# Products of zeros on TensorE, a broadcast of B written twice, and a second sum placed behind it, in a four-layer state-space network

## The chip, the cores and the metric

The kernel runs on one core of a Trainium2 chip. The metric is the device time of one execution in microseconds. The engines are TensorE (PE for matmuls, PEld for its weight loads), VectorE (DVE), ScalarE (ACT), GpSimd (POOL) and SyncE (SP), which issues the DMAs. Each engine takes its instructions in order.

## The reference, cut to what matters

Four layers, each a mixer with a residual and a small feed-forward network with a residual, run over four images of 64 x 64 tokens with 96 channels. The mixers of layers 1 to 3 are selective scans: from the image come 192 channels, read in four orders (rows, columns, and both backwards), and for each channel `d` of each order `k` there are 16 states `n`. Per layer:

```python
x_dbl = einsum('bkdl,kcd->bkcl', xs, x_proj_weight)
dts, Bs, Cs = split(x_dbl, [R, R + N], axis=2)
delta = softplus(einsum('bkrl,kdr->bkdl', dts, dt_projs_weight) + bias)
...
def step(h, inp):
    u_l, dl, b_l, c_l = inp
    dA = exp(dl[..., None] * A)
    h = dA * h + (dl * u_l)[..., None] * b_l[:, :, None, :]
    y = einsum('bkdn,bkn->bkd', h, c_l)
    return (h, y)
...
ys = ys + Dp * u
```

`b_l` and `c_l` depend on the order and the state, and not on the channel. The sum over `n` in `y` is a sum of 16 products. Around it stand a projection in, a 3 x 3 convolution, a layer norm, a gate and a projection out. Layer 0's mixer is another recurrence; the feed-forward networks quantise to 8 bits.

## The kernel before, in words

The kernel has three parts one after the other: layer 0 (`gated`, L1120), the scans of layers 1 to 3 (`scans`, L902), and the last image's end. The scans are the long part: 3 layers x 4 images make 12 stages, and a stage has 24 items: 2 directions x 4 segments of `T` = 1024 tokens x 3 chunks of 128 channels. An item has 16 tiles, one for each state, of 128 channels x 1024 tokens. That makes 288 items and 4608 tiles.

For each tile `k` the functions inside `scans` do this:

- `c_rows` (L931): two DMAs on SP's queue spread a row of C over 64 partitions each, into one of six `c` buffers.
- `decays` (L941): ScalarE takes the exponential, into `da`.
- `b_rows` (L947): TensorE spreads the row of B over 128 partitions, by two bf16 matmuls of 96 rows x 512 columns with the constant selector `sel`, into one of two PSUM buffers `bc` (`wide`, L136).
- `times_b` (L956): VectorE multiplies `du` into `bc`, in place.
- `scan` (L961): VectorE runs the recurrence along the tokens, into one of four `h` buffers.
- `carry` (L975): ScalarE keeps the last column for the next segment.
- `times_c` (L981): POOL multiplies `h` into `c`, in place.
- `accumulate` (L1001): TensorE adds the product to the item's sum `acc` in PSUM, by `add_quarters` (L986): four f32 matmuls, each on a quarter of the array. The trace shows each f32 matmul as two records, so eight a tile. The first state of an item first opens the sum with another such set. There is one `acc` buffer; `take` (L1012) copies it out on ScalarE, and `store` writes it to memory.

The loop (L1042) goes over pairs of tiles, `a` = 2j and `b` = 2j + 1; `m` is the pair's place in its item, 0 to 7. `InOrder` (L80) keeps each engine's instructions in the order in which the program gives them, so what is written first on an engine is first in its queue; all of its instructions show line L91. It also counts TensorE's work in `pe.columns`: columns streamed, an f32 matmul counted four times, a matmul on part of the array counted for its share (`columns`, L68).

Side work is the rest of the network: the projections of the items to come (`prepare_chunk`, `prepare_segment`) and, as `Job`s, the stretch between two layers of the next image. These are generators, and `beside` (L1072) moves them on twice in each pair, within a limit of columns (`PACE`, L77).

TensorE's queue in one pair is so: the sums of tiles `a - 4` and `b - 4`, the side work, the broadcast for `a + 2`, the broadcast for `b + 2`. On VectorE: `times_b(a)`, side work, `times_b(b)`, `scan(a)`, side work, `scan(b)`. A broadcast for `a + 2` may be written only when `scan(a)` has read the same buffer. The loads of C for `a + 2` and `b + 2` go into the buffers that the sums of `a - 4` and `b - 4` have read:

```python
for k in (a - 4, b - 4):
    if 0 <= k <= last:
        accumulate(k)
    if k + 6 <= last:
        c_rows(k + 6)
```

Of the kernel before, what the change touches and what calls it, by code (L numbers as in the profile page):

```python
# [12 lines left out]
BF16 = mybir.dt.bfloat16  # L13
# [13 lines left out]
MM = 512  # L27
# [10 lines left out]
NB3 = 96  # L38
# [35 lines left out]
    return n / (max(1, 128 // max(rows, 32)) * max(1, 128 // max(cols, 32)))  # L74


PACE = (2.0, 1600), (2.2, 1800), (2.6, 2000)  # L77


# [37 lines left out]
def metaformer(ctx: ExitStack, tc: tile.TileContext, x, l0_ab, l0_rest, ssm, ffn, out):  # L117
    nc = tc.nc
    pe, act, dve, pool, sp = (
        InOrder(tc, e) for e in (nc.tensor, nc.scalar, nc.vector, nc.gpsimd, nc.sync)  # L120
    )
# [6 lines left out]
    def sb(bufs, tag, shape, dtype=F32):  # L128
        return pools[bufs].tile(shape, dtype, tag=tag, name=tag)

    def const(name, shape, dtype=F32):
        return pools[1].tile(shape, dtype, name=name)
# [3 lines left out]
    def wide():  # L136
        return wides[0].tile([128, T], F32, tag="bc", name="bc")
# [11 lines left out]
    def settle():  # L149
        banks["free"] += banks["back"]  # L150
        banks["back"] = 0
# [20 lines left out]
    def drain(chain, others=lambda: None, until=lambda: False):  # L172

        while chain is not None and not chain.done and not until():
            if not pump(chain):
                others()
            settle()
# [16 lines left out]
    sel = const("sel", [NB3, NS, 128], BF16)  # L194
    for n in range(NS):
        for k in range(2):
            at = NS * k + n
            dve.tensor_copy(
                sel[:, n, 64 * k : 64 * k + 64], mod32[:, at : at + 1].to_broadcast([NB3, 64])
            )  # L200

    fold = const("fold", [128, 32])
    dve.tensor_tensor(fold, ident[:, 0:32], ident[:, 32:64], ALU.add)
# [9 lines left out]
    for layer in range(4):  # L213
# [8 lines left out]
        b = const(f"b_{layer}", [128, 3 + C])  # L222
# [538 lines left out]
    def slot():  # L761

        load["now"] = max(0, min(load["now"], 4 * load["most"]) - load["most"])
# [102 lines left out]
    def prepare_chunk(item):  # L866

        w, sg = weights[item.layer].w, item.sg
        i = 3 * item.d + item.chunk
        bias = w[:, W_DTB + i : W_DTB + i + 1]  # L870
        f = w[NB3 : NB3 + 2 * R, W_IN + 128 * i : W_IN + 128 * (i + 1)]


        delta, du = sb(2, "delta", [128, T]), sb(2, "du", [128, T])
        for k in range(2):
            cols = slice(k * MM, (k + 1) * MM)
            ps = bank("dt_proj")
            pe.matmul(ps, f, sg.rows[NB3 : NB3 + 2 * R, cols], start=True, stop=True)
            yield
            act.activation(delta[:, cols], ps, AF.Identity, bias=bias)  # L880
            release()
            yield k == 0
        act.activation(delta, delta, AF.Softplus)
        exp_and_ln()
        yield
        yield
        pool.tensor_tensor(du, delta, sg.us[item.chunk], ALU.mult)
        item.delta, item.du = delta, du
# [13 lines left out]
    def scans(stages, jobs, pac):  # L902
# [16 lines left out]
        tiles = [(i, n) for i in items for n in range(NS)]  # L919
        last = len(tiles) - 1  # L920
# [10 lines left out]
        def c_rows(k):  # L931
            i, n = tiles[k]
            c = live[k, "c"] = sb(6, "c", [128, T])
            for half in range(2):
                row = NS * half + n
                sp.dma_start(
                    out=c[64 * half : 64 * half + 64],
                    in_=i.sg.cs[row : row + 1, :].to_broadcast([64, T]),
                )
# [4 lines left out]
            at = (3 * i.d + i.chunk) * NS + n  # L944
            act.activation(da, i.delta, AF.Exp, scale=weights[i.layer].decay[:, at : at + 1])

        def b_rows(k):  # L947
            i, n = tiles[k]
            b = live[k, "b"] = wide()
            for half in range(2):  # L950
                cols = slice(half * MM, (half + 1) * MM)
                pe.matmul(
                    b[:, cols], sel[:, n, :], i.sg.bs[:, cols], start=True, stop=True
                )
# [31 lines left out]
        def add_quarters(i, v, lhs, start, stop):  # L986

            for k in range(2):
                for j in range(2):
                    p = slice(64 * j, 64 * j + 64)  # L990
                    o = 64 * (j ^ k)
                    pe.matmul(
                        i.acc[o : o + 64, j * MM : (j + 1) * MM],
                        lhs[p],
                        v[p, k * MM : (k + 1) * MM],
                        start=start,
                        stop=stop,
                        tile_position=(64 * j, o),
                    )

        def accumulate(k):  # L1001
            i, n = tiles[k]
            h = live.pop((k, "c"))
            if n == 0:
                i.acc = pac.tile([128, T], F32, tag="acc", name="acc")
                if i.d == 0:
                    add_quarters(i, i.sg.us[i.chunk], weights[i.layer].skip[:, i.chunk, :], True, False)
                else:
                    add_quarters(i, i.yf, stacked, True, False)
            add_quarters(i, h, stacked, False, n == NS - 1)  # L1010

        def take(i):  # L1012
            i.y = sb(2, "y", [128, T])
            act.copy(i.y, i.acc)
# [13 lines left out]
        for k in range(2):  # L1028
            c_rows(k)
            b_rows(k)  # L1030
# [10 lines left out]
        half = NS // 2  # L1041
        for j in range(len(tiles) // 2 + 2):  # L1042
            q, m = divmod(j, half)
            a, b = 2 * j, 2 * j + 1
            on = b <= last
            if on:
                item = items[q]
                nxt = at(q + 1)
                if m == 0:
                    if q % per == 0:  # L1050
                        item.im.y = dram.tile([3, 128, L], F32, tag="y", name="y")
                        working += jobs[q // per]
                    chain = None
                if m == 2 and nxt is not None:
                    if item.chunk == 2:
                        drain(segment, work, lambda: nxt.sg.steps)
                    chain = Chain(prepare_chunk(nxt), True)
                if item.chunk == 1 and m == 1 and at(q + 2) is not None:
                    if q % per == per - 2:
                        for job in jobs[q // per][:1]:  # L1060
                            while not job.done:
                                job.step()
                                settle()
                    segment = Chain(next_segment(items[q + 2 : q + 5]))
                if m == 4 and nxt is not None:
                    start(nxt)
                    if nxt.d == 1:
                        nxt.yf = sb(2, "y", [128, T])
                        t = slice(nxt.seg * T, (nxt.seg + 1) * T)
                        sp.dma_start(out=nxt.yf, in_=nxt.im.y[nxt.chunk, :, t])  # L1070

            def beside(n):  # L1072
                slot()
                pumped(chain)
                pumped(segment)
                if n == 13:
                    drain(chain, work)
                    if item.chunk == 2:
                        drain(segment, work)
                work(True)  # L1080
                settle()

            if on:
                decays(b)
            for k in (a - 2, b - 2):
                if 0 <= k <= last:
                    carry(k)
            if a + 2 <= last:
                decays(a + 2)
            if 0 <= b - 2 <= last:  # L1090
                times_c(b - 2)
                del live[a - 2, "h"], live[b - 2, "h"]
            for k in (a - 4, b - 4):
                if 0 <= k <= last:
                    accumulate(k)
                if k + 6 <= last:
                    c_rows(k + 6)
            if on:
                times_b(a)
            beside(2 * m)  # L1100
            if on:
                times_b(b)
                scan(a)
            beside(2 * m + 1)
            if a + 2 <= last:
                b_rows(a + 2)
            if on:
                times_c(a)
                scan(b)
            if b + 2 <= last:  # L1110
                b_rows(b + 2)
            if m == 1 and q >= 1:
                take(items[q - 1])
                store(items[q - 1])
# [241 lines left out]
    with tc.tile_pool(name="pbig", bufs=2, space=bass.MemoryType.PSUM) as wides_pool:  # L1356
# [5 lines left out]
        for at in range(len(stages)):  # L1362
            jobs.append([])
            if at + 1 < len(stages):
                im, layer = stages[at + 1]
                jobs[-1].append(Job(between(im, layer - 1), *PACE[layer > 1]))

            for im in {10: images[:2], 11: images[2:3]}.get(at, ()):
                jobs[-1].append(Job(between(im, 3, im.dst), *PACE[2]))
        with tc.tile_pool(name="pac", bufs=1, space=bass.MemoryType.PSUM) as pac:  # L1370
# [121 lines left out]
```

## Time and profile before

| | |
|---|---|
| three runs | 19366.18, 19418.11, 19423.85 us; median 19418.11 |
| the profiled execution's time | 19356.33 us |
| its span, first to last instruction | 19354.5 us |
| mean granted TensorE clock | 0.823 |
| layer 0, scans, end (us from the span's start) | 0 to 1704, 1704 to 19041, 19041 to 19355 |
| granted clock in these | 0.94, 0.82, 0.52 |
| busy, share of the span | PE 77%, DVE 90%, ACT 55%, POOL 70% |
| busy in the scans, of 17337 us | PE 13076, DVE 16205, ACT 9846, POOL 12711 us |
| loads of C | 9216, issue to landing 4.5 us |
| SP's wait for TensorE's sums | 8929.2 us, 2964 times |

The groups of instructions give the busy time of each operation and the idle time of its engine just before it, with what ended most of that. The waits give the same by pairs of waiter and releaser. The busy time in given stretches has the granted clock of each. The order of time gives start and duration, with instructions of one kind merged (x2 is two of them, from the first one's start to the last one's end).

### The profile page before, as it was taken

To read this page: it belongs to the slowest core of one execution; us is meant where nothing else is said; L and a number is where in the kernel's file an instruction comes from. 1 tells how busy PE (TensorE), PEld (TensorE's weight loads), DVE (VectorE), ACT (ScalarE), POOL (GpSimd) and SP (SyncE) were. 2 spreads that over 40 slices of the span, in tenths; PEclk is the share of its full clock that TensorE was granted. 3 is DMA by queue.
4 is the path that set the end of the run, shared out by engine and by line. 5 is a ranking of instruction groups with operands and counts; after the bars stand their busy time and mean duration, and the time that the engine had idled before them with its cause. 6 is when DMAs were issued, how large, how long until landed. Compare 5 with 4: busy or idle time off the path is not lost.

```text
span 19354.5 us, 236828 instructions
## 1 busy us (share of the span) xinstructions
PE 14811.6 (77%) x75584; PEld 4774.9 (25%) x75584; DVE 17417.6 (90%) x13768; ACT 10683.2 (55%) x17977; POOL 13500.1 (70%) x9220
## 2 busy tenths in 40 slices
PE   8897776776777777777777777777777777777777
PEld 3332121221222222222222222222222222222224
DVE  7668999999999999999999999999999999998994
ACT  3444565565555565565565565565565565565554
POOL 3435777777777777777777777777777777777774
PEclk9898887887887787787887887787887887787876
DMA  2123676676677667667677677667667677677773
GB/s 54 49 60 99 171 189 171 173 189 169 177 191 179 174 179 182 174 180 186 173 181 182 173 182 180 170 180 183 173 180 182 173 180 182 172 182 177 180 179 92
DMA packets 1269928, 3193.12 MB, mean 165 GB/s; under 512 B 440336, under 2 KB 440560, under 8 KB 1262544
## 3 DMA queue, kind: packets, MB, share of 16 engines
q1 hardware_dynamic: 1268688, 3177.97, 64.7%
q8 instruction: 609, 9.98, 0.2%
q14 instruction: 631, 5.17, 0.1%
HBM read 2818.51 MB, written 308.28 MB: 162 GB/s over the span
## 4 chain that ended last, share of the span: by engine, by line
issue 35%; PE 22%; DVE 20%; ACT 6%; DMA 4%; POOL 3%; SPq 1%; POOLq 0%; DVEq 0%; ACTq 0%
DVE h L91 13%; PE acc L91 11%; DVE bc L91 5%; PE bc L91 4%; POOL c L91 2%; PE y_t L91 2%; ACT L91 2%; PE dt_proj L91 1%; DMA c<-cs 1%; ACT da L91 1%; ACT u L91 1%; PE out_proj L91 1%; DVE st L91 1%; SPq L91 1%; DMA u<-u 1%
## 5 line engine op out<-in xcount | busy, mean ns | idle before, releaser
L91 POOL TENSOR_TENSOR c<-h,c 128x1024 f32<-128x1024 f32 (+1 forms) x4992 | 11281.7, 2276 | 4576.5 <-DVE h L91 1847.5
L91 DVE TENSOR_TENSOR_SCAN h<-da,carry,bc 128x1024 f32<-128x1024 f32 x4608 | 10585.8, 2331 | 263.6 <-ACT da L91 205.4
L91 ACT ACTIVATE da<-delta,decay 128x1024 f32<-128x1024 f32 x4608 | 5262.1, 1146 | 2266.5 <-DVE h L91 2256.8
L91 PE MATMUL acc<-c,twice 64*64 64x512 f32 x36864 | 6192.7, 801 | 52.9 <-POOL c L91 52.9
L91 DVE TENSOR_TENSOR bc<-du,bc 128x1024 f32<-128x1024 f32 x4608 | 5475.3, 1216 | 737.2 <-PE bc L91 722.3
L91 PE MATMUL bc<-bs,sel 96*128 96x512 bf16 x9216 | 3171.1, 440 | 3619.7 <-DVE h L91 3518.2
L91 PEld LDWEIGHTS acc<-c,twice 64*64 64x64 f32 x36864 | 1550.1, 172 | 3485.6 <-issue 2661.7
L91 PEld LDWEIGHTS <-sel 96*128 96x128 bf16 x9216 | 639.4, 102 | 5978.4 <-DVE h L91 5470.6
L91 ACT ACTIVATE delta<-dt_proj,w 128x512 f32<-128x512 f32 x576 | 394.4, 685 | 1547.2 <-PE dt_proj L91 1546.0
L91 ACT COPY carry<-h 128x1 f32<-128x1 f32 x3456 | 580.0, 184 | 1080.5 <-DVE h L91 1076.2
L91 ACT ACT_TABLE_LOAD x857 | 1099.5, 1283 | 15.7 <-PEq L1485 0.7
L91 PE MATMUL conv<-pad,taps 64*64 64x256 f32 (+1 forms) x9216 | 781.8, 393 | 42.4 <-ACT u L91 33.3
L91 POOL TENSOR_TENSOR du<-delta,u 128x1024 f32<-128x1024 f32 x288 | 678.3, 2355 | 16.1 <-ACT delta L91 14.6
L91 PE MATMUL x_proj<-u,xp 128*108 128x512 f32 x1152 | 632.3, 660 | 62.3 <-DMA u<-u 34.5
L91 PE MATMUL dt_proj<-rows,w 12*128 12x512 f32 x1152 | 669.7, 662 | 3.7 <-ACT u L91 2.7
L91 ACT ACTIVATE c<-c,l_bias 128x512 f32<-128x512 f32 x384 | 263.8, 687 | 726.8 <-PE c L91 716.8
L91 PEld LDWEIGHTS conv<-pad,taps 64*64 64x64 f32 (+1 forms) x9216 | 430.4, 142 | 600.5 <-issue 387.7
L91 DVE TENSOR_TENSOR_SCAN h<-da,l_carry,bc 128x512 f32<-128x512 f32 x384 | 491.4, 1280 | 41.0 <-DVE bc L91 1.4
L91 POOL CAST hq<-ff_h 128x512 fp8e5<-128x512 f16 x384 | 233.3, 611 | 326.7 <-ACT ff_h L91 326.6
L91 PE MATMUL y_t<-ident,pad 128*128 128x128 f32 (+1 forms) x1536 | 401.8, 348 | 54.2 <-DMA pad<-y 46.8
L91 ACT COPY u<-conv 64x256 f32<-64x256 f32 x768 | 280.6, 365 | 241.7 <-PE conv L91 143.3
L91 PE MATMUL bc<-rows,u 96*128 96x512 f32 x768 | 391.8, 635 | 28.2 <-DVE h L91 27.5
(138 smaller groups left out, 11927.0 us busy)
## 6 DMA issues: line engine op xcount, KB each, us to landing
c<-cs SPq DMA_DIRECT2D x9216, 256.0 KB, 4.5
u<-u SPq DMA_DIRECT2D x288, 512.0 KB, 6.8
y<-y SPq DMA_DIRECT2D x1152, 128.0 KB, 4.2
y<-y SPq DMA_DIRECT2D x144, 512.0 KB, 6.4
xr<-x SPq DMA_DIRECT2D x224, 192.0 KB, 5.3
u<-u SPq DMA_DIRECT2D x288, 128.0 KB, 4.0
pad<-y SPq DMA_DIRECT2D x288, 128.0 KB, 5.8
z<-zl SPq DMA_DIRECT2D x96, 256.0 KB, 4.8
```

The lines of the kernel that those rows point to most:

```text
L91: ins = f(*a, **k).ins
```

## The change

Three edits, all in the scans:

- `b_rows` gets a count. The first tile's broadcast is written twice into the same buffer (four matmuls, the last two with the same values as the first two); the second tile's once, as before.
- The sum of `b - 4` and the loads of C for `b + 2`, which follow it in the program, are placed behind the broadcast for `a + 2`. The sum of `a - 4` and the loads for `a + 2` stay where they were.
- `keep_busy` adds products of a constant of zeros (96 x 128, bf16) with `sel` to the open sum of tile `a - 4`'s item, 512 columns each, alternating between the sum's two halves. They stand behind the side work and ahead of the broadcast for `a + 2`. Their number is what is missing from 4608 columns, counting the side work's columns in this pair, in whole products of 512; a pair without side work gets nine.

TensorE's queue in one pair is then: the sum of `a - 4`, the side work, the products of zeros, the broadcast for `a + 2` twice, the sum of `b - 4`, the broadcast for `b + 2`.

```diff
+FILL = 4608
 PACE = (2.0, 1600), (2.2, 1800), (2.6, 2000)
...
+    nothing = const("nothing", [NB3, 128], BF16)
+    pool.memset(nothing, 0.0)
...
-        def b_rows(k):
+        def b_rows(k, times=1):
             i, n = tiles[k]
             b = live[k, "b"] = wide()
-            for half in range(2):
-                cols = slice(half * MM, (half + 1) * MM)
+            for half in range(2 * times):
+                cols = slice(half % 2 * MM, (half % 2 + 1) * MM)
                 pe.matmul(
                     b[:, cols], sel[:, n, :], i.sg.bs[:, cols], start=True, stop=True
                 )
...
+        def keep_busy(i, n):
+
+            for j in range(n):
+                pe.matmul(
+                    i.acc[:, j % 2 * MM : (j % 2 + 1) * MM],
+                    nothing,
+                    sel[:, 0 : MM // 128, :],
+                    start=False,
+                    stop=False,
+                )
...
-            for k in (a - 4, b - 4):
-                if 0 <= k <= last:
-                    accumulate(k)
-                if k + 6 <= last:
-                    c_rows(k + 6)
+            if 0 <= a - 4 <= last:
+                accumulate(a - 4)
+            if a + 2 <= last:
+                c_rows(a + 2)
+            before = pe.columns
             if on:
                 times_b(a)
             beside(2 * m)
...
             beside(2 * m + 1)
+            if 0 <= a - 4 <= last:
+                keep_busy(tiles[a - 4][0], max(0, FILL - int(pe.columns - before)) // MM)
             if a + 2 <= last:
-                b_rows(a + 2)
+                b_rows(a + 2, 2)
+            if 0 <= b - 4 <= last:
+                accumulate(b - 4)
+            if b + 2 <= last:
+                c_rows(b + 2)
             if on:
                 times_c(a)
                 scan(b)
```

## The prediction

> **What bounds the kernel now.** I read the page first, then the granted clock, the waits, the busy time in short windows and the order of time. In the page (line engine op, names, shapes, count | busy us, mean ns | idle before it, by whom):
>
> ```profile
> PEclk9898887887887787787887887787887887787876
> L91 DVE TENSOR_TENSOR_SCAN h<-da,carry,bc 128x1024 f32<-128x1024 f32 x4608 | 10585.8, 2331 | 263.6 <-ACT da L91 205.4
> L91 PE MATMUL acc<-c,twice 64*64 64x512 f32 x36864 | 6192.7, 801 | 52.9 <-POOL c L91 52.9
> L91 DVE TENSOR_TENSOR bc<-du,bc 128x1024 f32<-128x1024 f32 x4608 | 5475.3, 1216 | 737.2 <-PE bc L91 722.3
> ```
>
> VectorE's two operations on each of the 4608 tiles set the time. The scans run from 1704 to 19041 us, 17,337 us for 2304 pairs of tiles. A pair with nothing else on VectorE takes 6.74 us, in all 15,520 us; VectorE's side work adds 731 us and its idle time the rest. The change can win idle time alone: 722 us are waits for TensorE's broadcast of B, 205 us waits for ScalarE's decay. The waits, us in total, times, longest:
>
> ```profile
> PE bc L91 <- DVE h L91: 3576.9, 2638, 16.5
> ...
> DVE bc L91 <- PE bc L91: 722.3, 494, 17.9
> ```
>
> TensorE itself idles 3577 us for VectorE, as a broadcast may be written only when the scan has read that buffer; so it is late only in some pairs. All 494 waits are at the first tile of a pair, whose broadcast stands behind two sums and the side work. The clock decides which. Its record has two values, 1.00 and 0.50, and changes at multiples of 3.41 us. Such windows in a stretch without side work (PE busy first, granted clock before DMA share):
>
> ```profile
> 3081.84:3085.25 3.41, 1.43 (x10) 0.11 (x2) 3.41 (x2) 2.78 (x3) 1.87 (x1) 1.00 0.58 156
> 3085.25:3088.67 3.42, 3.13 (x14) 0.93 (x18) 3.42 (x4) 1.15 (x1) 3.42 (x3) 0.50 0.65 151
> 3088.67:3092.08 3.41, 1.43 (x10) 0.11 (x2) 3.41 (x2) 1.15 (x1) 3.41 (x2) 1.00 0.61 165
> 3092.08:3095.49 3.41, 3.10 (x14) 0.93 (x18) 3.40 (x4) 1.15 (x1) 2.92 (x2) 0.50 0.54 143
> ```
>
> After a full-clock window with 1.43 us of work comes one at half clock; after a half-clock window with 3.1 us, one at full. A stretch that keeps the clock:
>
> ```profile
> 8246.21:8249.63 3.42, 1.84 (x14) 0.63 (x18) 3.42 (x3) 2.39 (x5) 3.42 (x2) 1.00 1.02 253
> 8249.63:8253.04 3.41, 3.27 (x26) 1.07 (x18) 3.41 (x3) 3.37 (x4) 1.36 (x2) 1.00 0.77 220
> 8253.04:8256.45 3.41, 1.92 (x18) 0.67 (x20) 3.41 (x3) 3.39 (x8) 3.41 (x2) 1.00 0.59 139
> ```
>
> Here 1.84 us holds it. Over the scans' 5079 windows (1867 at half clock), 813 of 818 full-clock windows with PE busy under half were followed by a fall, 198 of 397 at 0.5 to 0.6, 174 of 1997 above. Counted in columns streamed (a 512-column bf16 product is 512, a sum 2048), the fall comes below about 3250 in a window. It costs: of the 2302 pairs counted, 873 had the full clock ahead of their broadcast and 43 us of waits, the others 684 us. The durations, in order of time:
>
> ```profile
> 8241.05 0.60 PE L91 MATMUL bc<-bs,sel 96*128 96x512 bf16 x2 [1.63 <-DVE h L91]
> ...
> 8241.59 1.95 PE L91 MATMUL acc<-c,twice 64*64 64x512 f32 x16
> ...
> 9014.41 1.04 PE L91 MATMUL bc<-bs,sel 96*128 96x512 bf16 x4
> ...
> 9022.22 1.03 PE L91 MATMUL bc<-bs,sel 96*128 96x512 bf16 x2 [1.90 <-DVE h L91]
> 9023.18 3.69 PE L91 MATMUL acc<-c,twice 64*64 64x512 f32 x16
> ```
>
> At full clock a broadcast takes 0.60 us, two sums 1.95, four broadcast products 1.04, so a further product 0.22; at half clock 1.03, 3.69 and, as 1.03 less a single product's 0.60 (the longest row has 634 ns), 0.43.
>
> **The change, part by part.**
>
> *Products of zeros.* Side work between two pairs' broadcasts, counted from the matmul rows, averages 2541 columns; 215 pairs have none. The filling to 4608 gives 9334 products, 4.05 a pair, 9 in an empty one: 9334 x 0.22 = 2053 us at full clock. Each one's weight load (102 ns in the row of the loads from sel) lies beside it.
>
> *Second write of B.* 2304 x 2 x 0.22 = 1014 us. In a plain pair at full clock TensorE then works 1.95 + 1.04 + 0.60 + 9 x 0.22 = 5.57 of 6.74 us, so both lie in the 3577 us of idle time; that cover goes at half clock: 3.69 + (1.03 + 0.86) + 1.03 + 9 x 0.43 = 10.48 us.
>
> *Second sum behind the broadcast.* It takes 0.9 us at full clock out of the way of the first tile's broadcast and stands before the second's. Plain pair, full clock, first scan's end as zero: broadcast 0.06 to 1.1, sum to 2.0, second broadcast from the second scan's end, 2.3, to 3.0, when VectorE wants it at 3.4. At half clock the same chain is 1.9, 3.7, 4.7: a wait of 1.2 us that no pair has now.
>
> *Together, the clock left as it is.* For each pair I set the broadcast's start to the later of the scan's end and the end of the side work, added its time to the last write (0.63 us, written twice 1.06), and counted what this ends after VectorE is free; the moved sum takes 0.85 us off the side work's end, each fill adds 0.21. Today's order gives 673 us so (722 measured). The move alone gives 310, with the double write 449, with the fills at full-clock price 758. So the work added eats the move; only the clock can pay.
>
> *What the clock does.* The emptiest window of a plain pair now holds four broadcast products and a sum: 4 x 512 + 2048 = 4096 columns, about 1.95 us of PE busy between gaps of 1.1 and 0.3 us, above both 3250 and the 1.84 that held. Without the second write it would be 3072, below. So the falls that come of waiting for a scan should go. In 993 of 1184 such falls that wait was the largest gap; 191 came of side work that waits for other engines, and no fill stands inside those gaps. To these I add about 150 for VectorE's side work ahead of the first scan (177 pairs with over 0.8 us) and for transposes, whose columns count for less: 340 falls. Each takes 3.41 us x half = 1.7 us of TensorE's work from a pair with some 1.2 to spare, or makes the 1.2 us wait above: between 0 and 1.7, taken as 1.0, near the 1.2. Today it is 684 / 1184 = 0.58 us.
>
> *The rule of the skill.* The Trainium skill, "TensorE: Matmul & The Clock Gate", section "Why this matters for your kernels", asks for no idle gaps over about 3 us between bursts. No gap in the plain stretch is that long (1.63 us before a broadcast in the rows above), so by the rule its clock would never fall, the fills would buy nothing, and the profiled time would be 85 us (758 less 673) longer, near 19,440. The windows at 0.50 contradict it, and the measurement decides.
>
> *Loads of C and the copy of the sum.* The second tile's c buffer is freed by the moved sum, so its two loads issue about 2.8 us later (from 0.75 us before the scan's end to 2.1 after), past the side work's DMAs in SP's queue. They land a median 5.1 us ahead of POOL's product now, 2.9 at the tenth percentile: some 230 tiles come late, by about 1 us. Behind that product POOL holds the next ones and side work; its 4600 us of idle time in the scans cover it: 0, or 230 us without. Next in SP's queue are the first tile's loads, which wait for a later sum anyway. ScalarE's copy of the finished sum (1.04 us, 288 times) waits until 2 us after the scan; behind it the next decay is wanted 4 us later: 0. The zeros' memset is one instruction beside the loads at the start.
>
> *The sum.* Waits for B: 45 us in the 873 full-clock pairs by the new order, x 2304 / 873 = 119; with 340 x 1.0 it is 459, a gain of 263 us (bounds: 119 + 0, gain 603; 119 + 340 x 1.7 = 697, gain 25). ScalarE's decay is late behind results of TensorE; a third of its 205 us, 60, goes (0 to 100). 19,356 - 323 = **19,033** for the profiled execution, 62 us under the median shown; for a median about **19,100**.
>
> **The rivals.**
>
> *Full clock nearly throughout.* Waits 119, decay gain 100: 19,356 - 703 = 18,653, at the median 18,715. For it: 4096 against 3250. Against it: the 191 falls.
>
> *TensorE becomes the bound.* If zeros, or a sum with a broadcast, don't hold the clock, each pair pays 10.48 us at half clock. With today's 37% of windows a plain pair takes 0.63 x 5.57 + 0.37 x 10.48 = 7.39 us, 0.65 over 6.74, times 2304 = 1500 us, in place of the 722: 20,134, at the median 20,200. It decides from the share where 5.57 + 4.91 x = 6.74, 24% of windows. For it: the added work alone costs more than the move gives. Against: a full array leads back to the full clock (1135 of 1240 half-clock windows over 0.9 busy).
>
> *The wait moves.* It goes from the first tile to the second, or to POOL through C: nothing measured, 19,360 to 19,480. For it: the 758 against 673.
>
> **How the numbers follow.** The forecast, about 18,850 to 19,330: 0.50. Full clock, below that: 0.15. The wait moves: 0.10. TensorE the bound, from 19,480: 0.25, more often part of its price than all. The range 18,650 to 19,850 leaves out the worse half of that rival. A measurement can tell about 0.3% from no change: faster 0.66, same 0.08, slower 0.26.
>
> **What would show it.** Granted clock in the scans from 0.82 to about 0.95; plain stretches at 1.00 in each window; 13,824 broadcast products and some 9300 of zeros at 0.22 us; VectorE's wait for B near 460 us, some of it now at second tiles. Wrong if windows with 4096 columns are followed by 0.50, if VectorE waits over 722 us, or if POOL's wait for C grows by more than 230 us.

## The result, and the profile after

The changed kernel took 19,704.09 us (median of four runs, 19,666.04 to 19,724.13) beside 19,393.35 us for the kernel before (four runs, 19,366.18 to 19,423.85): a ratio of 1.0157, 95% interval 1.0132 to 1.0183. It is slower by 1.6%; the forecast was 19,100 us, faster. The profiled execution has a span of 19,699.8 us and a mean granted clock of 0.927 in place of 0.823.

The page of the changed kernel, the clock in 40 slices and the groups (columns as before; all of `InOrder`'s instructions now show line L92):

```profile
PEclk9898999999999999999999999999998999998996
...
L92 DVE TENSOR_TENSOR_SCAN h<-da,carry,bc 128x1024 f32<-128x1024 f32 x4608 | 10589.3, 2333 | 290.8 <-ACT da L92 184.7
...
L92 DVE TENSOR_TENSOR bc<-du,bc 128x1024 f32<-128x1024 f32 x4608 | 5468.0, 1215 | 1115.9 <-PE bc L92 1105.3
L92 PE MATMUL bc<-bs,sel 96*128 96x512 bf16 x13822 | 4086.1, 408 | 1732.8 <-DVE h L92 1710.5
L92 PE MATMUL acc<-c,twice 64*64 64x512 f32 x36864 | 5328.0, 649 | 24.0 <-POOL c L92 23.9
...
L92 PE MATMUL acc<-sel,nothing 96*128 96x512 bf16 x8684 | 2432.4, 404 | 0.0
```

VectorE's own work is what it was (10,589 and 5468 us in the two groups). The clock is up and the sums are shorter (mean 649 ns a record, 801 before), so the change does to TensorE what it says. Yet VectorE waits 1105 us for the broadcast of B in place of 722. The waits of the changed kernel (total us, times, longest):

```profile
ACT y L92 <- PE acc L92: 1139.0, 254, 9.4
DVE bc L92 <- PE bc L92: 1105.3, 725, 12.3
POOL c L92 <- DMA c<-cs: 871.3, 288, 17.4
```

Of the 1105 us, 757 are in 275 waits at first tiles and 348 in 450 waits at second tiles, where there were none. The two others grew as well: ScalarE's wait for the sum from 192 to 1139 us, POOL's for its loads of C from 353 to 871. VectorE hardly feels them: its wait for ScalarE's decay is 185 us (205 before), for POOL 84 us (36).

The profiled execution is 345 us longer than the one before. 304 us of it lie in the scans (17,339 to 17,643 us): VectorE's idle time ahead of the products with B grew by 382 us, and it won some 75 us of other idle and busy time back. Another 45 us lie in layer 0, in which nothing was changed (the scans begin at 1749 us in place of 1704).

Busy time in windows of 3.41 us, changed kernel, in a plain stretch (PE busy first, granted clock before the DMA share):

```profile
3151.71:3155.12 3.41, 3.23 (x21) 1.02 (x18) 3.41 (x4) 1.15 (x1) 3.41 (x3) 1.00 0.45 129
3155.12:3158.53 3.41, 2.58 (x15) 0.62 (x13) 3.41 (x2) 1.15 (x1) 3.41 (x2) 1.00 0.73 183
3158.53:3161.95 3.42, 3.24 (x22) 1.06 (x19) 3.42 (x4) 1.15 (x1) 3.05 (x2) 1.00 0.58 146
3161.95:3165.36 3.41, 2.58 (x15) 0.57 (x13) 3.41 (x2) 1.15 (x1) 1.95 (x1) 1.00 0.68 162
```

This is the stretch of the prediction's windows at 1.00 and 0.50, and now each window has the full clock. The loss lies elsewhere. The same pair of tiles in both kernels shows it. In order of time, the kernel before:

```profile
6630.20 4.57 DVE L91 TENSOR_TENSOR_SCAN h<-da,carry,bc 128x1024 f32<-128x1024 f32 x2
...
6632.37 0.21 PE L91 MATMUL ff_y<-w,hq 128*128 128x96 fp8e5 x1
...
6634.47 1.17 POOL L91 CAST hq<-ff_h 128x512 fp8e5<-128x512 f16 x2
...
6635.13 0.26 PE L91 MATMUL ff_y<-w,hq 128*128 128x96 fp8e5 x1 [2.55 <-POOL hq L91]
...
6635.69 0.50 PE L91 MATMUL ff_y<-w,hq 128*128 128x96 fp8e5 x4 [0.30 <-POOL hq L91]
...
6635.99 1.91 PE L91 MATMUL bc<-bs,sel 96*128 96x512 bf16 x4
...
6637.08 2.36 DVE L91 TENSOR_TENSOR bc<-du,bc 128x1024 f32<-128x1024 f32 x2 [2.31 <-PE bc L91]
```

and the changed kernel:

```profile
6735.40 0.21 PE L92 MATMUL ff_y<-w,hq 128*128 128x96 fp8e5 x1
6735.73 4.57 DVE L92 TENSOR_TENSOR_SCAN h<-da,carry,bc 128x1024 f32<-128x1024 f32 x2
...
6739.99 1.16 POOL L92 CAST hq<-ff_h 128x512 fp8e5<-128x512 f16 x2
...
6740.65 0.26 PE L92 MATMUL ff_y<-w,hq 128*128 128x96 fp8e5 x1 [5.04 <-POOL hq L92]
...
6741.21 0.50 PE L92 MATMUL ff_y<-w,hq 128*128 128x96 fp8e5 x4 [0.29 <-POOL hq L92]
...
6741.51 2.76 PE L92 MATMUL acc<-sel,nothing 96*128 96x512 bf16 x6
...
6744.06 1.91 PE L92 MATMUL bc<-bs,sel 96*128 96x512 bf16 x4
...
6745.91 1.99 PE L92 MATMUL acc<-c,twice 64*64 64x512 f32 x8
6746.02 1.23 DVE L92 TENSOR_TENSOR bc<-du,bc 128x1024 f32<-128x1024 f32 x1 [5.71 <-PE bc L92]
...
6747.83 1.03 PE L92 MATMUL bc<-bs,sel 96*128 96x512 bf16 x2
...
6748.90 1.23 DVE L92 TENSOR_TENSOR bc<-du,bc 128x1024 f32<-128x1024 f32 x1 [1.65 <-PE bc L92]
```

TensorE's side work waits here for POOL's cast `hq`. The wait ends at the same place in the pair in both kernels, 4.9 us after the start of the pair's first scan. With the sum moved away and the clock full, TensorE comes to it 2.5 us sooner (0.1 us ahead of that start in place of 2.4 behind it) and sits idle 5.04 us in place of 2.55. At the next boundary the clock falls, to half for 10.24 us (6.83 in the kernel before). Then six products of zeros (2.76 us) and a broadcast written twice (1.91 us) stand between the cast and VectorE, and the moved sum stands ahead of the second tile's broadcast. VectorE waits 5.71 + 1.65 us where it waited 2.31.

**All falls, by cause.** I call a change of the granted clock from 1.00 to 0.50 in the scans a fall. Each is sorted by TensorE's longest kind of idle time in the window ahead of it, a wait for a scan or a wait of side work, and is given VectorE's waits for B until 8 us after its end or the next fall. Falls without such an idle time (12 before, 22 after), and waits outside these stretches (34 of the 1105 us in the changed kernel), are left out:

| kernel | falls: scan, each | falls: side work, each |
|---|---|---|
| before | 993, 0.42 us | 181, 1.61 us |
| changed | 134, 1.01 us | 226, 3.98 us |

The change took away 859 falls that cost little (677 of the 993 cost no wait over 0.15 us, the least that is counted), some 280 us together: 993 x 0.42 less 134 x 1.01. The falls of side work are more in number and dearer: 226 x 3.98 less 181 x 1.61 is 608 us.

### The profile page after: what moved, and what is told of

Its sections match the earlier page's. It is cut to its first block, busy times and chain, and to the rows that moved or that the text cites. A ratio compares the mean times of both kernels' runs of the same rounds, so it can differ in the third digit from the quotient of the medians.

```text
span 19699.8 us, 263158 instructions
## 1 busy us (share of the span) xinstructions
PE 16687.5 (85%) x88874; PEld 5429.4 (28%) x88874; DVE 17383.1 (88%) x13768; ACT 10723.2 (54%) x17977; POOL 13504.0 (69%) x9221
## 5 line engine op out<-in xcount | busy, mean ns | idle before, releaser
L92 POOL TENSOR_TENSOR c<-h,c 128x1024 f32<-128x1024 f32 (+1 forms) x4992 | 11288.1, 2277 | 5007.9 <-DVE h L92 2198.4
L92 DVE TENSOR_TENSOR_SCAN h<-da,carry,bc 128x1024 f32<-128x1024 f32 x4608 | 10589.3, 2333 | 290.8 <-ACT da L92 184.7
L92 ACT ACTIVATE da<-delta,decay 128x1024 f32<-128x1024 f32 x4608 | 5267.3, 1146 | 2805.5 <-DVE h L92 2798.7
L92 DVE TENSOR_TENSOR bc<-du,bc 128x1024 f32<-128x1024 f32 x4608 | 5468.0, 1215 | 1115.9 <-PE bc L92 1105.3
L92 PE MATMUL bc<-bs,sel 96*128 96x512 bf16 x13822 | 4086.1, 408 | 1732.8 <-DVE h L92 1710.5
L92 PE MATMUL acc<-c,twice 64*64 64x512 f32 x36864 | 5328.0, 649 | 24.0 <-POOL c L92 23.9
L92 PEld LDWEIGHTS <-sel 96*128 96x128 bf16 x13822 | 1087.2, 101 | 5544.4 <-DVE h L92 4258.7
L92 PE MATMUL acc<-sel,nothing 96*128 96x512 bf16 x8684 | 2432.4, 404 | 0.0
L92 PEld LDWEIGHTS acc<-c,twice 64*64 64x64 f32 x36864 | 1032.3, 138 | 2209.0 <-issue 1545.4
L92 ACT COPY carry<-h 128x1 f32<-128x1 f32 x3456 | 589.7, 183 | 1190.0 <-DVE h L92 1187.1
L92 PEld LDWEIGHTS <-nothing 96*128 96x128 bf16 x8684 | 799.2, 102 | 1551.7 <-issue 982.1
L92 ACT COPY y<-acc 128x1024 f32<-128x1024 f32 x288 | 291.5, 1012 | 1179.8 <-PE acc L92 1139.0
L92 PE MATMUL conv<-pad,taps 64*64 64x256 f32 (+1 forms) x9216 | 768.1, 387 | 89.1 <-ACT u L92 50.2
L92 ACT ACTIVATE delta<-dt_proj,w 128x512 f32<-128x512 f32 x576 | 394.4, 685 | 784.5 <-PE dt_proj L92 783.2
L92 POOL TENSOR_TENSOR du<-delta,u 128x1024 f32<-128x1024 f32 x288 | 677.7, 2353 | 16.9 <-ACT delta L92 15.4
L92 ACT ACTIVATE c<-c,l_bias 128x512 f32<-128x512 f32 x384 | 263.7, 687 | 761.3 <-PE c L92 753.2
L92 PE MATMUL x_proj<-u,xp 128*108 128x512 f32 x1152 | 605.8, 636 | 73.1 <-DMA u<-u 36.5
L92 PE MATMUL dt_proj<-rows,w 12*128 12x512 f32 x1152 | 650.4, 644 | 16.2 <-ACT u L92 14.9
L92 PEld LDWEIGHTS conv<-pad,taps 64*64 64x64 f32 (+1 forms) x9216 | 415.1, 135 | 562.5 <-issue 295.7
L92 DVE TENSOR_TENSOR_SCAN h<-da,l_carry,bc 128x512 f32<-128x512 f32 x384 | 491.4, 1280 | 41.0 <-DVE bc L92 1.4
L92 PE MATMUL bc<-rows,u 96*128 96x512 f32 x768 | 404.0, 652 | 28.6 <-DVE h L92 27.9
```

Of the source, the lines that this page charges most:

```text
L92: ins = f(*a, **k).ins
```

## The experiments

Each ratio is to the kernel before on the same chip, with its 95% interval. "First" and "second" are VectorE's waits for B at the first and second tile of a pair, in us; clock and falls are of the profiled execution.

| run | median us | ratio | clock | falls | first | second |
|---|---|---|---|---|---|---|
| before | | 1 | 0.823 | 1186 | 722 | 0 |
| changed | 19,704 | 1.0157 (1.0132 to 1.0183) | 0.927 | 382 | 757 | 348 |
| e1 move | 19,496 | 1.0044 (1.0030 to 1.0058) | 0.832 | 873 | 343 | 490 |
| e2 move, double | 19,712 | 1.0159 (1.0141 to 1.0178) | 0.870 | 859 | 397 | 683 |
| e3 zeros | 19,694 | 1.0149 (1.0130 to 1.0169) | 0.859 | 955 | 1069 | 0 |
| e4 double | 19,589 | 1.0094 (1.0077 to 1.0111) | 0.846 | 989 | 925 | 0 |
| e5 move, zeros | 19,631 | 1.0115 (1.0098 to 1.0132) | 0.902 | 528 | 634 | 395 |
| e6 ones | 19,731 | 1.0168 (1.0152 to 1.0183) | 0.925 | 385 | 755 | 338 |
| e7 zeros first | 19,662 | 1.0131 (1.0113 to 1.0148) | 0.925 | 466 | 509 | 463 |
| e8 half move | 19,370 | 0.9981 (0.9966 to 0.9997) | 0.825 | 902 | 514 | 142 |
| e9 changed, rounds | 19,655 | 1.0121 (1.0107 to 1.0135) | 0.929 | 366 | 741 | 316 |
| e10 before, rounds | 19,322 | 0.9952 (0.9938 to 0.9965) | 0.827 | 1166 | 633 | 0 |
| e11 half move, rounds | 19,358 | 0.9971 (0.9959 to 0.9982) | 0.822 | 952 | 523 | 125 |
| e12 zeros in empty pairs | 19,575 | 1.0081 (1.0065 to 1.0097) | 0.891 | 689 | 388 | 537 |
| e13 before, jobs first | 22,927 | 1.1812 (1.1794 to 1.1830) | 0.741 | 1569 | 193 | 0 |
| e14 changed, jobs first | 22,701 | 1.1695 (1.1679 to 1.1711) | 0.899 | 171 | 37 | 53 |
| e15 rounds, empty pairs | 19,339 | 0.9968 (0.9957 to 0.9979) | 0.838 | 1140 | 662 | 0 |

### The parts one by one: e1 to e5

e1, the move alone:

```diff
-FILL = 4608
+FILL = 0
...
-                b_rows(a + 2, 2)
+                b_rows(a + 2)
```

> Only the second sum (with its loads of C) moves behind the first tile's broadcast; no products of zeros, one write of B. Theory (the waits come at falls of the clock, and each fall is dear because of the work added): without the added work a half-clock pair needs 3.69 + 2 x 1.03 us and stays under its 6.74, so falls stay near the 1186 of before but stay cheap; waits at first tiles fall from 722 toward the 310 us worked out for the move, second tiles get up to 300: 19,150 to 19,400 us. Rival (the move itself costs, by waits at second tiles and by late loads of C): the 348 us at second tiles and the 871 us of POOL's wait for C of the changed kernel stay, 19,500 us or more.

The first tiles went as worked out, 722 to 343 us (310 in the sum). The second tiles did not: 490 us, over the 300 that the theory allowed, and the run is nearer to the rival. The order of time of e1 at half clock:

```profile
3090.54 1.03 PE L92 MATMUL bc<-bs,sel 96*128 96x512 bf16 x2 [3.72 <-DVE h L92]
3091.50 1.99 PE L92 MATMUL acc<-c,twice 64*64 64x512 f32 x8
3093.42 1.03 PE L92 MATMUL bc<-bs,sel 96*128 96x512 bf16 x2
...
3094.49 1.23 DVE L92 TENSOR_TENSOR bc<-du,bc 128x1024 f32<-128x1024 f32 x1 [0.65 <-PE bc L92]
```

Broadcast, sum and broadcast follow each other without a gap, 3.9 us, and VectorE waits 0.65 us at the second tile. So the move costs in itself while the clock is at half.

e2, the move and the double write (the first of the two edits above):

> The move and the double write, no products of zeros. Theory: one of the two emptiest windows of a plain pair holds 4096 columns, but the other only a broadcast, a sum and what side work there is, 3072 and up, so the clock stays between the two kernels (0.83 to 0.90), with 600 to 1000 falls, and waits between 600 and 900 us: 19,300 to 19,550. Rival (the products of zeros alone make the loss): as fast as the move alone or faster. Rival (the move or the double write make it): as slow as the changed kernel, 19,700.

The theory's time was missed, 19,712 in place of 19,550 at most, and the waits are 1080 us. The second tiles have 683 us: the double write stands ahead of the moved sum too. The second rival was right: without a single product of zeros the kernel is as slow as the changed one (1.0159 and 1.0157). The zeros take falls away (859 to 382) and make those that stay dearer, and the two cancel.

e5, the move and the zeros (the second of the two edits):

> The move and the products of zeros, B written once. Theory: the window between the two scans' ends holds 1024 + 2048 = 3072 columns, under some 3250, so plain pairs fall again: 700 falls or more, each with the long queue of zeros: 19,900 to 20,300 us, slower than the changed kernel. Rival (more work on TensorE is what costs, clock or not): 2304 x 0.44 us less of it, so faster than the changed kernel, 19,500 to 19,650.

Missed: the rival was right, 528 falls and faster than the changed kernel. The window that I had put at 3072 columns holds the clock more often than thought. The second write takes the falls from 528 to 382 and still makes the kernel slower by 0.4%. Sorted as above, a fall of side work cost 1.6 us before, 2.0 in e1, 2.7 in e2, 3.2 in e5 and 4.0 in the changed kernel: each part that is added raises its price.

e3, the zeros alone, and e4, the double write alone, have both sums ahead of the side work again:

```diff
-            if 0 <= a - 4 <= last:
-                accumulate(a - 4)
-            if a + 2 <= last:
-                c_rows(a + 2)
+            for k in (a - 4, b - 4):
+                if 0 <= k <= last:
+                    accumulate(k)
+                if k + 6 <= last:
+                    c_rows(k + 6)
...
-            if 0 <= a - 4 <= last:
+            if 0 <= a - 4 <= last and m != 1:
                 keep_busy(tiles[a - 4][0], max(0, FILL - int(pe.columns - before)) // MM)
...
-            if 0 <= b - 4 <= last:
-                accumulate(b - 4)
-            if b + 2 <= last:
-                c_rows(b + 2)
```

e3 has this and `b_rows(a + 2)`; e4 has it with `FILL = 0` and `b_rows(a + 2, 2)`.

> Products of zeros alone: both sums ahead of the side work as before, B written once, the zeros behind the side work (none in the pair in which an item's sum is closed, one of eight). Theory (at a fall of the clock the whole queue ahead of the broadcast is paid twice): a plain pair holds the clock also so, as only the gap of 1.6 us between the broadcasts is left; falls below 600; no waits at second tiles; but sums, side work and zeros all stand ahead of the first tile's broadcast, 3.69 + 3.87 us at half clock, so 2 to 3 us a fall there: waits for B 900 to 1200 us, 19,500 to 19,750. Rival (the move is what makes the added work dear): waits under 722 us, faster than before.

> The double write alone, in the old order, no zeros. Theory: each late broadcast is late by a further 0.43 to 0.86 us, and pairs that had just enough room become late: waits at first tiles 1000 to 1150 us, none at second tiles, 19,600 to 19,800; falls somewhat fewer than 1186. Rival (the double write costs only through the moved sum that stands behind it, as move and double write together gave 683 us at second tiles): 19,400 to 19,500.

e3's time and waits (1069 us) came as expected, its falls did not (955, not under 600). e4 is 0.94% slower, below the range of the theory but far over the rival's 19,500. So each part is slower by itself, and the second write's price needs no moved sum behind it.

### The values and the place of the zeros: e6, e7, e12

```diff
-    pool.memset(nothing, 0.0)
+    pool.memset(nothing, 1.0)
```

> The changed kernel with the constant set to one in place of zero, so that the sums take wrong values added and the output is not the reference's. Theory that zeros count for less toward the clock (a fit over the windows of the changed kernel gives about 4000 columns of zeros where 2900 to 3200 of sums or broadcasts hold it): clock above 0.927, falls below 300, time 100 us or more under the changed kernel. Rival (the values do not matter): clock 0.927, 382 falls and the time of the changed kernel within 0.3%.

Clock 0.925 and 385 falls: it does not matter whether the constant is zero or one, the rival was right.

e7 puts four products ahead of the side work:

```diff
-            before = pe.columns
+            if 0 <= a - 4 <= last:
+                keep_busy(tiles[a - 4][0], 4)
...
-            if 0 <= a - 4 <= last:
-                keep_busy(tiles[a - 4][0], max(0, FILL - int(pe.columns - before)) // MM)
```

> The changed kernel with the products of zeros ahead of the side work in place of behind it, four in each pair (9208 in all, against 8684 behind it). Theory (the falls that are left come of side work that waits for POOL or ScalarE, and zeros behind late side work delay the broadcast when it is late already; ahead of it they run while it would wait): falls near 382, under 2.5 us of waits for each in place of 2.8, waits for B 700 to 950 us, 19,350 to 19,600. Rival (each column in the queue costs the same wherever it stands): waits near 1105 us, 19,650 to 19,750.

First tiles 757 to 509 us, and falls of side work at 3.04 us each in place of 3.98; but second tiles 348 to 463, more falls (466), and the time stays in the rival's range. The place matters for the price of a fall, and little for the total.

e12 keeps the zeros only where a pair has no side work (1989 products):

```diff
-                keep_busy(tiles[a - 4][0], max(0, FILL - int(pe.columns - before)) // MM)
+                keep_busy(tiles[a - 4][0], FILL // MM if pe.columns == before else 0)
```

> The changed kernel with the products of zeros only in pairs without any side work, nine in each, some 1900 in place of 8684. Theory (zeros behind side work that is late make the remaining falls dear): falls after side work's waits fall from 4.0 us each to about the 2.7 of move and double write without zeros; falls of waiting for a scan lie between 134 and 614; waits for B 850 to 1050 us, 19,500 to 19,680. Rival (the double write and the move are what makes them dear, not the zeros): 4.0 us each as with all zeros, and more falls, 19,750 or more.

As the theory had it: some 230 falls of side work at 2.55 us, 440 of waiting for a scan, 925 us, 0.8% slower than before in place of 1.6%. It is faster than e2, which has no zeros. So beside the move and the double write, zeros where nothing waits gain, and the other 6700 lose that again.

### Taking away causes: e8 to e11, e15

e8 moves half of the second sum, without zeros or second write:

```diff
-        def accumulate(k):
+        def accumulate(k, lo=0, hi=MM):
...
+            if 0 <= b - 4 <= last:
+                accumulate(b - 4, 0, MM // 2)
...
             if a + 2 <= last:
                 b_rows(a + 2)
+            if 0 <= b - 4 <= last:
+                accumulate(b - 4, MM // 2)
+            if b + 2 <= last:
+                c_rows(b + 2)
```

> No zeros, B written once, and only half of the second sum (256 of each 512 columns, with its loads of C) moved behind the first tile's broadcast. Theory (the move costs at second tiles because broadcast, sum and broadcast at half clock, 1.03 + 1.99 + 1.03 us, are more than the 3.4 us that VectorE leaves; half a sum gives 3.1): waits at second tiles under 100 us, at first tiles about half way from 731 to 351, 540 us; 19,150 to 19,300, faster than before. Rival (the price at second tiles comes of loads of C or of changing between whole and quartered array): second tiles keep 200 us or more, 19,350 or more.

Second tiles 490 to 142 us, first tiles 514. It is faster than before by 0.2%, which is less than expected: the time lies in the rival's range, the waits at second tiles between the two. The half that fits at half clock costs little; what it gains is small too.

e9 and e10 let three more rounds of side work pass ahead of the wait shown above, in the changed kernel and in the one before; e11 does it in e8:

```diff
         pool.tensor_copy(hq[:, 2, :], late, saturate=False)
-        yield
+        for _ in range(4):
+            yield
         yield True
```

> The changed kernel with three more rounds of side work between POOL's last cast of the hidden layer and the matmuls of the feed-forward network's second layer, so that TensorE meets them later and waits less for POOL. Theory (the 226 falls that are left come of side work that waits for other engines, and cost 4.0 us each with the added work): the 43 falls whose longest gap is this wait, with 175 us of VectorE's waits, go for the most part: 100 to 175 us faster than the changed kernel, 19,530 to 19,600. Rival (a fall comes anyway a little later, or the late broadcasts have other causes): within 50 us of the changed kernel.

> The same three rounds in the kernel before. Theory: the same 48 falls cost 78 us there (1.6 each), so 40 to 80 us less, 19,320 to 19,360: half or less of what the same edit gives in the changed kernel. Rival (the price of such a fall does not hang on the work added): as large a gain as in the changed kernel.

> Half of the second sum moved, no zeros, B written once, with the same three rounds. Theory: the gain of the half move (0.2%, waits for B 656 us) and that of the rounds add up: waits near 590 us, 19,280 to 19,340, faster than before. Rival: the rounds make the stages' side work end later and the gain is lost, 19,370 or more.

TensorE's wait for `hq` fell as meant (207 to 27 us in e9). In e9 the falls of side work were 226 again: others took their place, 3.89 us each, and the gain is 0.36% by the ratios (1.0157 to 1.0121), some 50 to 70 us, under the 100 expected. In e10 they went from 181 to about 140 and the time fell by 0.48%, more than expected; the expectation that the edit would give twice as much in the changed kernel was not borne out. e10 beats both kernels and has the lowest median of all runs, though the intervals of e11 and e15 overlap with its own. In e11 the two gains did not add.

e15 is e10 with nine zeros in pairs without side work, in the old order:

> The old order with B written once, the three further rounds ahead of the second layer of the feed-forward network (0.48% faster than before by itself), and nine products of zeros only in pairs without any side work. Theory: falls of waiting for a scan drop from 1014 to about 850 and take 50 to 80 us of VectorE's waits with them: 19,240 to 19,290. Rival (those falls cost nothing, and zeros at half clock make the next broadcast late): 19,320 or more.

The falls of waiting for a scan went from 1014 only to 977, and the kernel is not faster than e10. Those falls had cost 0.34 us each there: nothing to be gained from them.

### Without the next image's side work beside the scans: e13 and e14

```diff
-                        working += jobs[q // per]
+                        for job in jobs[q // per]:
+                            job.finish()
```

> The kernel before with the next image's side work of each stage run through ahead of the stage's scans in place of beside them (only the items' own projections stay beside them). It is the partner of the run below and longer than the kernel before by what no longer lies beside the scans. Theory (VectorE waits for B where side work stands ahead of the broadcast at half clock): in the scans' pairs waits for B under 250 us, though the clock falls as often as before or more, since falls of empty pairs cost nothing. Rival (half clock itself costs): waits near 722 us or more.

> The changed kernel with the side work run ahead in the same way. Theory (the change loses because the falls that are left come of side work that waits, and the added work stands in the queue then): without side work the clock holds in nearly all pairs, few falls are left, waits for B within 100 us of the partner's, and the time within 0.5% of the partner's in place of 1.6% over it. Rival (the added work or the move costs in itself): 1% or more over the partner.

The waits for B, e13 first:

```profile
DVE bc L91 <- PE bc L91: 192.8, 246, 2.7
```

```profile
DVE bc L92 <- PE bc L92: 90.1, 91, 3.3
```

The theory held, and by more than expected: here the change is faster, 22,701 to 22,927 us, 1.0%. In e13 the clock fell 1569 times and cost 193 us of counted waits; the 1450 or so falls of waiting for a scan cost 0.11 us each, and 1219 of them nothing that is counted. In e14 171 falls are left. The median pair takes 6.74 us in place of 6.85, as a second broadcast at half clock ends about 0.1 us late, too little to be counted as a wait (those under 0.15 us are not). In e13 VectorE starts the second tile's product 1.2 us behind the first's in place of 1.12 in 1138 pairs, some 100 us in all, and in e14 in hardly any: with the 103 us of counted waits that is most of the 226 us. The kernel before has 505 such pairs, some 45 us, so its falls of waiting for a scan were cheap, but not quite free.

So where the next image's side work is taken away, the added work and the move cost less (90 us of waits in all) than the steady clock wins, and with it they lose 1.6%. The two runs take away both that work's waits for other engines and its columns in TensorE's queue; which of the two makes the falls dear they do not tell.

## Why the prediction was wrong

- **What bounds the kernel:** right. VectorE's busy time in the scans stayed (16,205 and 16,172 us), its wait for B decided.
- **Zeros and second write lie in TensorE's idle time at full clock:** right in plain stretches (windows at 1.00) and in e14. The page shows 8684 zeros where I counted 9334; why is not shown.
- **Together, the clock left as it is:** half wrong. For the first tiles the move gave 343 us where 310 was worked out. The sum left the second tiles out; I had named their 1.2 us at half clock one paragraph earlier and put them only into the price of a fall. e1 measured 490 us there: the move alone is a loss of 0.4%, not a gain.
- **What the clock does:** right for the change as a whole: 382 falls where 340 were forecast, clock 0.93 in the scans where 0.95 was, and of 1311 full-clock windows that held only the scans' products, with 4000 columns or more, one led to a fall. That the second write is needed for it was not: without it, in e5, some 280 falls of waiting for a scan are left of 993. The rule on idle gaps of the Trainium skill ("TensorE: Matmul & The Clock Gate", "Why this matters for your kernels") does not tell the two kernels apart: the stretch had no gap over 1.63 us before and went between 1.00 and 0.50, and kept 1.00 once its windows were filled.
- **The price of a fall:** the step that failed. I took 1.0 us, between 0 and 1.7. Measured: 1105 us in 382 falls, 2.9 each. There were two faults. I started from the mean of today's falls, 0.58 us, while the falls that the change removes are the cheap ones (0.42) and those that it leaves cost 1.61 already. And the upper bound took one lost window, 3.41 us: a fall lasts 684 x 3.41 / 382 = 6.1 us on average, one of side work 7.1, two windows, and zeros, second write and sum all stand in the queue at half clock, 3.98 us a fall of side work. With 226 x 3.98 + 134 x 1.01 in place of 340 x 1.0 the sum would have been 119 + 1035 = 1154, near the 1105 measured.
- **Loads of C:** POOL's wait grew by 518 us, over the 230 that I had set as a limit; the cover held nearly, with 48 us more of VectorE's waits for POOL.
- **ScalarE:** the copy of the sum cost no time, as forecast. Of the 60 us to be gained at the decay, 20 came.
- **The rivals:** the time ended on the side of "TensorE becomes the bound", but not by its mechanism: 684 of 5180 windows at half clock are 13%, under the 24% from which it decides. In stretches such as the one shown above, behind a late wait, TensorE is the bound. "The wait moves" named the second tiles and priced them at nothing.

What is left open: e9 shows that taking one cause of late side work away from the changed kernel brings others forward, and not which waits would all have to go.

## What to carry to other kernels

Work added to keep a clock up is free only where nothing queued behind it is ever late: price it in the stretches where the clock will fall all the same, at the lower clock, behind the late work. Sort the stalls by cause before multiplying a count by a mean price: the cheap ones may be those that the change removes. An in-order engine that is made faster comes to its next wait sooner and waits longer there; putting other work ahead of that wait (e10, 0.48% faster) was worth more than all that was done to its clock.

## What the runs showed of the hardware

- The columns streamed in a window tell what the clock does next, in the kernel before with a sharp edge. I take windows that hold only broadcasts and sums, counted as in the prediction. Of those at full clock all 448 under 3250 columns were followed by a fall, 15 of 30 up to 3500, and none of 224 above. Of those at half clock 444 of 448 under 3250 stayed at half, and all 640 over 3500 went to full.
- Products with ones and with zeros held the clock alike: 0.925 with 385 falls, 0.927 with 382. Both count for less than the same columns of broadcasts and sums. Of the changed kernel's full-clock windows with 3500 to 4000 columns, 15 of 17 that held some zeros were followed by a fall and none of 29 without; with ones 20 of 22 and none of 24. In e5 it was 12 of 101 and none of 78, so how much less they count is not shown.
- The way back to the full clock is less sure in the changed kernel. Of half-clock windows over 0.9 busy, 1135 of 1240 led to it before and 375 of 533 in the changed kernel, and a fall lasts 6.1 us on average in place of 5.4 (1867 x 3.41 / 1186). The falls that are left are mostly of side work, which lasted longer before too (6.2 us).
- Of full-clock windows with PE busy 0.55 to 0.6, 7 of 92 led to a fall in the changed kernel, and 61 of 173 before. How busy the matmul rows look does not alone decide it.
